# Queries and keys of the second layer by 15 products of two by three by three parts, in two passes of three heads

## The chip, the cores and the metric

The kernel runs on one core of a Trainium2 chip. The metric is device time in microseconds, median of the runs shown. The engines are named as in the profile: PE is TensorE's matmul, PEld its weight load, DVE VectorE, ACT ScalarE, POOL GpSimd, SP the sync engine; SPq is SP's queue, from which every DMA of this kernel is issued.

## The reference

Two layers of graph attention run on 128 graphs of 64 nodes with 768 features, all in float32. What follows is cut to what matters here.

```python
# layer 0: 12 heads of 64, additive attention, gate; then
x = _layernorm(x + layer0(x, adj, ...))
# layer 1: 6 heads of 128
q = _heads(x @ Wq + bq); k = _heads(x @ Wk + bk); v = _heads(x @ Wv + bv)
scores = einsum('bhqd,bhkd->bhqk', q, k) / sqrt(128)
probs = softmax(scores + where(graph_mask, 0, NEG), axis=-1)
ctx = einsum('bhqk,bhkd->bhqd', probs, v)          # heads side by side again
x = _layernorm(x + ctx @ Wf + bf)
```

## The kernel before, in words

The 8,192 tokens are 64 tiles of 128, which are 32 pairs and 16 **quads** of 512 tokens. There are two phases.

**Phase A** (`phase_a`) does layer 0 and the values of layer 1, a pair at a time: `hidden` (h), `gate` (g) and, two pairs late, `value` (v). Each is a product of a 256 x 768 by a 768 x 768 matrix in two by two by two parts with seven products instead of eight (`TURNS`, `by_token`); sums of token blocks (`x_sums`) and of weight blocks (T1 to N4) are made beforehand. Around them `attend` runs the attention of layer 0 on the other engines, each step at a time of its own (`KEYS`). At a pair's end `away` writes x1, transposed, and its four sums to `ops_there` in DRAM, seven blocks in all. In the last pair the matrices of queries and keys are loaded into the places of those no longer needed, and their sums made (`matrix`: four sums in three pieces each).

**Phase B** (`phase_b`) does layer 1, a quad at a time. Its pieces are:

- `queries(q, f)` and `keys(q, f)` for f = 0, 1, 2, each through `by_feature`: seven products of three matmul calls, 128 features by 256 tokens each, which give two heads (f and f + 3) for the quad's 512 tokens. ACT and DVE read the sums out of PSUM into `zone`, with the bias. The operands lie in `zone` as seven blocks, loaded by `load_block` from `ops_there`; the next quad's loads go out as the last keys use the blocks up.
- `slab(Q, f)`: the scores of two heads (s_ps, in PSUM), softmax, the turning of the weights by a copy on ACT, a DMA transpose and two copies back (sT), the context (c_ps), and then for each of two heads a copy into `parts`, a DMA transpose and copies into cT. `parts` has two buffers. In the third slab, right behind the context, `load` issues eight loads of the next quad's values.
- `operands(Q, i)` and `output(Q, i)` for i = 0, 1: the product with Wf for half the tokens of a quad, in two by three by three parts with 15 products (`FIFTEEN`) of two calls each. DVE makes eleven sums of context blocks (sc, L1102) and adds each product to the rows (y, L1148). An accumulator in PSUM is used for several products, and is written on only when the one before has been read.
- `rows_of` loads x1 rows into y, and POOL adds the bias bf; `normed` does the last norm.

The order on each engine is that in which the program emits instructions. It is planned by `Beat`, a clock of the program itself: a product is emitted, its read follows one and a half lengths later, and started lines (`slab`, `operands`, `rows_of`) emit a step whenever their time has come. Every engine works through its own instructions in this order. A quad's three steps f each emit queries, keys and the start of slab f; the output of the quad before follows the keys of f = 1 (i = 0) and of f = 2 (i = 1).

Of the kernel before, what the change touches and what calls it, by code (L numbers as in the profile page):

```python
# [45 lines left out]
F32 = mybir.dt.float32  # L46
# [3 lines left out]
ALU = mybir.AluOpType  # L50
# [24 lines left out]
PLACES = {X11: 0, X12: 1, X22: 2, S1: 3, S2: 4, S3: 5, S4: 6}  # L75

IN_ZONE = {X11: 0, S2: 1, S1: 2, X12: 3, S4: 4, X22: 5, S3: 6}
# [19 lines left out]
    (3, "A5", 3, ((1, 3),)),  # L97
    (1, "A3", 1, ((1, 4),)),
    (0, "2", 11, ((-1, 3),)),
    (4, "14", 2, ((1, 2),)),  # L100
# [5 lines left out]
    (5, "6", 13, ((-1, 4),)),  # L106
    (1, "0", 10, ((1, 5),)),
)

# [99 lines left out]
def two_layers(  # L209
# [68 lines left out]
    def matrix(w, name, engine, gap):  # L278

        t = places[place[name]]  # L280
        blocks = w.rearrange("(k c p) (m n) -> k m p c n", k=2, p=P, m=2)
        for at, k, m in ((W11, 0, 0), (T3, 0, 1), (W22, 1, 1), (W21, 1, 0)):
            for c in range(KH):
                nc.sync.dma_start(t[:, at, c], blocks[k, m][:, c])
                yield gap
        yield 3
        for to, a, b in ((T1, T3, W11), (T2, W22, T1), (T3, W22, T3), (N4, W21, T2)):
            for c in range(KH):
                engine.tensor_tensor(t[:, to, c], t[:, a, c], t[:, b, c], ALU.subtract)
                yield gap  # L290
        ready[f"{name}_sb"] = t
# [85 lines left out]
    ops_there = [dram.tile([P, 2, 7 * KH, P], F32, name=f"ops_there_{q}") for q in range(n_quads)]  # L377
# [3 lines left out]
    zone = const.tile([P, 7 * KH * 2 * P + 8 * P * 2], F32, name="zone")  # L381
# [10 lines left out]
    def load_block(q, k):  # L392

        at = PLACES[k] * KH
        t = in_zone(IN_ZONE[k] * D, KH, 2, P)
        for i in range(2):
            nc.sync.dma_start(t[:, :, i, :], ops_there[q][:, i, at : at + KH, :])
        return t.rearrange("p c i t -> p c (i t)")

    def queries(q, f, blocks, part):  # L400
        quads[q]["qT"] = in_zone(7 * KH * 2 * P, 2, 4 * P)
        by_feature(f"q_{q}_{f}_", blocks, ready["wq_sb"], f, bq_sb, quads[q]["qT"], part)

    def keys(q, f, blocks, part, then=None):
        quads[q]["kT"] = in_zone((7 * KH + 4) * 2 * P, 2, 4 * P)
        by_feature(f"k_{q}_{f}_", blocks, ready["wk_sb"], f, bk_sb, quads[q]["kT"], part, then)

    def by_feature(name, blocks, w, f, b_sb, r, part, then=None):

        sums = [sb(dense[0], [P, BANK], "dense", f"{name}{i}") for i in range(3)]  # L410
        begun = set()
        lo, hi = b_sb[:, f : f + 1], b_sb[:, f + 3 : f + 4]
        T = 2 * P
        u = {}

        def more(i, ps):
            u[i] = part(f"{name}u{i}")[:, 0:T]
            nc.vector.tensor_tensor(u[i], u[1], ps, ALU.add)

        def p1(ps):  # L420
            u[1] = part(f"{name}u1")[:, 0:T]
            nc.scalar.copy(u[1], ps)  # L422

        def p2(ps):
            nc.scalar.activation(r[:, 0, 0:T], ps, AF.Identity, bias=lo)

        def p7(ps):
            nc.vector.scalar_tensor_tensor(r[:, 1, T : 2 * T], ps, hi, u[3], ALU.add, ALU.add)

        def p4(ps):  # L430
            nc.vector.scalar_tensor_tensor(r[:, 0, T : 2 * T], ps, lo, u[1], ALU.add, ALU.add)

        def p3(ps):
            nc.vector.scalar_tensor_tensor(r[:, 1, 0:T], ps, hi, u[2], ALU.add, ALU.add)

        reads = dict(P1=p1, P2=p2, P3=p3, P4=p4, P5=lambda ps: more(3, ps), P6=lambda ps: more(2, ps), P7=p7)
        for what, to, xb, wb in TURNS:
            ps = sums[to][:, 0:T]

            def emit():  # L440
                for c in range(KH):
                    nc.tensor.matmul(  # L442
                        ps,
                        lhsT=w[:, wb, c, f * P : (f + 1) * P],
                        rhs=blocks[xb][:, c, :],
                        start=(c == 0 and to not in begun),
                        stop=(c == KH - 1),
                        skip_group_check=True,
                    )

            read = reads[what]
            beat.product(emit, lambda read=read, ps=ps: read(ps))
            begun.add(to)
            if then:
                then(xb)

    def phase_a(pa, ps_a, dst_pool):
# [25 lines left out]
        w_dst_sb = row(w_dst, "w_dst_sb", pa)  # L485
# [4 lines left out]
        w_src_sb = row(w_src, "w_src_sb", pa)  # L490
        h_b_sb = row(h_b, "h_b_sb", pa)
# [17 lines left out]
        h_of_tile = [pa.tile([P, H0, EP], F32, name=f"h_{i}") for i in range(3)]  # L509
        hx_of = [pa.tile([P, 6, EP], F32, name=f"hx_{i}") for i in range(2)]  # L510
# [299 lines left out]
        def sums_of_pair(p, begin):  # L810
# [12 lines left out]
            def away():  # L823
                there = ops_there[p // 2][:, p % 2]
                nc.sync.dma_start(there[:, 0 : 2 * KH], xo[:, 0:2].rearrange("p k c t -> p (k c) t"))
                nc.sync.dma_start(there[:, 2 * KH : 3 * KH], xo[:, 3])
                nc.sync.dma_start(there[:, 3 * KH : 7 * KH], so.rearrange("p k c t -> p (k c) t"))
# [26 lines left out]
        for p in range(n_pairs):  # L854
# [15 lines left out]
            if p + 1 == n_pairs:  # L870
                beat.start(matrix(wq, "wq", nc.gpsimd, 0.6), 7)
                beat.start(matrix(wk, "wk", nc.vector, 0.6), 14)
# [6 lines left out]
        def first_blocks():  # L879
            for _, _, xb, _ in TURNS:  # L880
                blocks[xb] = load_block(0, xb)
                yield 1

        beat.start(first_blocks())
        value(n_pairs - 2)
        beat.until(lambda: len(blocks) == 7)
        beat.until(lambda: "wq_sb" in ready)
        queries(0, 0, blocks, part)
        beat.until(lambda: "wk_sb" in ready)
        keys(0, 0, blocks, part)  # L890
# [16 lines left out]
    def phase_b(pb, ps_b):  # L907
        bf_sb = row(bf, "bf_sb", pb)


        wf_sb = places[place["wf"]].rearrange("p a b c -> p (a b c)")[:, 0 : 15 * 2 * THIRD]
        wf_sb = wf_sb.rearrange("p (a c n) -> p a c n", a=15, c=2)

        def last_matrix():
            blocks = wf.rearrange("(c k p) (m n) -> k m p c n", k=3, p=P, m=3)
            for k in range(3):
                for m in range(3):
                    nc.sync.dma_start(wf_sb[:, 3 * k + m], blocks[k, m])
                    yield 1
            yield 4  # L920
            for m in range(3):
                last_bias(m)
                yield 1
            ready["bias"] = bf_sb

            for to, a, b, op in (
                (9, 0, 7, ALU.add),
                (10, 5, 8, ALU.add),
                (11, 3, 7, ALU.subtract),
                (12, 3, 8, ALU.subtract),  # L930
                (13, 4, 7, ALU.add),
                (14, 1, 2, ALU.subtract),
                (1, 1, 4, ALU.add),
                (1, 1, 9, ALU.add),
                (4, 14, 13, ALU.add),
# [318 lines left out]
```

## Time and profile before

| | |
|---|---|
| median of 3 runs | 2865.06 us (2863.92 to 2869.85) |
| the profiled execution's own time | 2868.3 us |
| its span, first to last instruction | 2866.4 us |
| mean granted TensorE clock | 0.994 |
| PE busy, phase A 100 to 1300 us | 1198.80 of 1200 us |
| PE busy, phase B 1600 to 2750 us | 1141.88 of 1150 us |
| DVE, ACT, POOL busy, 1600 to 2750 us | 661.10, 399.93, 136.01 us |
| one quad of phase B, 2401.60 to 2490.30 us | 88.7 us, PE busy 87.91, DVE 51.55, ACT 30.90, POOL 10.75 |
| last product of the keys to the end | 2806.94 to 2866.4 us |

Busy time on an engine that is not the bottleneck costs nothing by itself. A group's line names the source line, the engine, the operation, what is written and read, the count, the busy time, the mean length, and the idle time in front with what ended it. A float32 matmul call shows as two PE instructions.

### The profile page before, as it was taken

Reading aid. Unit: us, or ns where it says so; the run is one execution under the profiler, and the core shown is the slowest. Engines: PE = TensorE matmul, PEld = TensorE weight load, DVE = VectorE, ACT = ScalarE, POOL = GpSimd, SP = SyncE. Lnnn points to the kernel's source line nnn. Section 1 sums busy time; section 2 is a strip of 40 time slices with the busy share of each in tenths; the row PEclk is TensorE's granted clock in tenths of the full one; section 3 lists DMA queues with packets and bytes.
Section 4 is the critical chain, followed back from the end, with each engine's and each line's share of the span. In section 5 each row is a group of like instructions: output and inputs, shape, how many; then the busy total and the mean of one; then the engine's idle time right before and its main releaser. Section 6 shows DMA issues by size and latency. Waiting matters only on the chain.

```text
span 2866.4 us, 43840 instructions
## 1 busy us (share of the span) xinstructions
PE 2804.1 (98%) x16168; PEld 2038.1 (71%) x16168; DVE 2039.1 (71%) x4103; ACT 1305.3 (46%) x1562; POOL 1067.2 (37%) x938
## 2 busy tenths in 40 slices
PE   7899999999999999999899999999999999999998
PEld 4455555555555555555588888888888888888886
DVE  6888888888888888888636555565555655556556
ACT  2655655665665665665423333333333333333331
POOL 6656656666665665665421101101011110110102
PEclk9999999999999999999999999999999999999999
DMA  6666666666666666667764445534355343554532
GB/s 205 152 175 170 175 168 169 179 165 170 182 163 172 179 165 170 186 160 193 195 156 116 106 100 131 135 87 117 86 130 135 90 120 84 127 135 94 128 82 63
DMA packets 627014, 409.61 MB, mean 143 GB/s; under 512 B 440176, under 2 KB 573040, under 8 KB 626800
## 3 DMA queue, kind: packets, MB, share of 16 engines
q1 hardware_dynamic: 626800, 406.81, 55.2%
q8 instruction: 128, 2.10, 0.3%
q14 instruction: 86, 0.70, 0.1%
HBM read 186.69 MB, written 119.93 MB: 107 GB/s over the span
## 4 chain that ended last, share of the span: by engine, by line
PE 89%; DMA 4%; DVE 2%; SPq 1%; ACT 1%; issue 1%; POOL 0%; POOLq 0%; ACTq 0%; DVEq 0%
PE v L346 15%; PE o L1135 15%; PE h L346 14%; PE g L346 14%; PE q L442 14%; PE k L442 12%; PE f_all L742 2%; PE s_ps L991 2%; PE c_ps L1047 2%; DMA out<-y 2%; DMA sT<-parts 2%; SPq L980 1%; ACT cT L1069 0%; PE bias_ps L951 0%; DMA s<-parts 0%
## 5 line engine op out<-in xcount | busy, mean ns | idle before, releaser
L370 POOL TENSOR_TENSOR rs<-rs,power 128x1 f32<-128x1 f32 x128 | 73.9, 577 | 1079.4 <-DVE rs L368 1079.4
L346 PE MATMUL h<-w,zone 128*128 128x384 f32 x1320 | 446.2, 494 | 21.7 <-ACT h L533 12.5
L442 PE MATMUL q<-zone,w 128*128 128x256 f32 x2016 | 461.6, 384 | 3.8 <-issue 1.2
L346 PE MATMUL g<-w,zone 128*128 128x384 f32 x1320 | 441.3, 489 | 4.4 <-DVE gate L587 3.3
L442 PE MATMUL k<-zone,w 128*128 128x256 f32 x2016 | 443.2, 379 | 0.9 <-ACT k_u L422 0.9
L442 PEld LDWEIGHTS q<-zone,w 128*128 128x128 f32 x2016 | 381.2, 191 | 63.5 <-issue 8.4
L442 PEld LDWEIGHTS k<-zone,w 128*128 128x128 f32 x2016 | 382.9, 190 | 53.4 <-ACT k_u L422 1.3
L346 PEld LDWEIGHTS h<-w,zone 128*128 128x128 f32 x1320 | 250.7, 192 | 194.6 <-ACT h L533 13.7
L346 PEld LDWEIGHTS g<-w,zone 128*128 128x128 f32 x1320 | 247.5, 190 | 176.4 <-DVE gate L587 12.8
L1135 PE MATMUL o<-w,sc 128*128 128x256 f32 x1364 | 326.7, 384 | 4.7 <-DVE sc L1102 4.7
L1148 DVE TENSOR_TENSOR y<-y,o 128x256 f32<-128x256 f32 x512 | 206.7, 415 | 126.7 <-PE o L1135 120.1
L1135 PEld LDWEIGHTS o<-w,sc 128*128 128x128 f32 x1364 | 256.1, 191 | 43.8 <-DVE sc L1102 6.0
L346 PE MATMUL v<-w,x_sums 128*128 128x384 f32 x768 | 258.5, 486 | 1.7 <-DVE x_sums L315 1.7
L1118 POOL TENSOR_TENSOR y<-y,bf_sb 128x768 f32<-128x768 f32 x64 | 118.4, 1865 | 342.4 <-DMA y<-x_there 313.9
L662 POOL TENSOR_TENSOR bc_e<-th_d,w_dst_sb 128x768 f32<-128x768 f32 x64 | 120.0, 1875 | 287.2 <-ACT th_d L557 267.6
L346 PEld LDWEIGHTS v<-w,x_sums 128*128 128x128 f32 x768 | 145.7, 190 | 104.0 <-DVE x_sums L315 3.0
L1161 ACT ACTIVATE y<-y,rs 128x768 f32<-128x768 f32 x64 | 65.7, 1026 | 157.8 <-POOL rs L371 157.8
L657 POOL TENSOR_SCALAR zone<-zone 128x768 f32<-128x768 f32 x64 | 137.3, 2146 | 0.0
L1009 ACT ACTIVATE s<-s 128x512 f32<-128x512 f32 x48 | 30.1, 626 | 226.2 <-DVE s L1007 226.2
L1102 DVE SCALAR_TENSOR_TENSOR sc<-cT 128x256 f32<-128x256 f32 x217 | 113.9, 525 | 22.9 <-ACT cT L1069 22.8
L650 ACT ACTIVATE gate<-gate 128x768 f32<-128x768 f32 x64 | 53.9, 843 | 166.8 <-DVE gate L593 118.5
L733 ACT COPY bc_e<-th_d 128x1536 uint16<-128x1536 uint16 x64 | 123.2, 1926 | 13.2 <-DMA th_d<-bc_e 13.2
(162 smaller groups left out, 4625.1 us busy)
## 6 DMA issues: line engine op xcount, KB each, us to landing
zone<-ops_there SPq DMA_DIRECT2D x224, 192.0 KB, 4.4
zone<-in_xT SPq DMA_DIRECT2D x32, 768.0 KB, 6.2
zone<-in_x SPq DMA_DIRECT2D x64, 384.0 KB, 3.9
bc_e<-there SPq DMA_DIRECT2D x128, 192.0 KB, 3.4
x_there<-mix SPq DMA_DIRECT2D x64, 384.0 KB, 4.2
ops_there<-x_sums SPq DMA_DIRECT2D x32, 768.0 KB, 3.3
v_there<-v SPq DMA_DIRECT2D x128, 192.0 KB, 2.6
v<-v_there SPq DMA_DIRECT2D x128, 192.0 KB, 3.9
```

Source lines behind the costliest of these rows:

```text
L346: nc.tensor.matmul(ps, lhsT=blocks[xb][:, c, :], rhs=w[:, wb, c, :], start=(c == 0 and to not in begun), stop=(c == KH - 1), skip_group_ch ...
L370: nc.gpsimd.tensor_tensor(rs[:, 0:1], rs[:, 0:1], power, ALU.pow)
L442: nc.tensor.matmul(ps, lhsT=w[:, wb, c, f * P : (f + 1) * P], rhs=blocks[xb][:, c, :], start=(c == 0 and to not in begun), stop=(c == KH - 1),
L657: nc.gpsimd.tensor_scalar(xs, xs, 1.0, None, ALU.add)
L662: nc.gpsimd.tensor_tensor(bc, th, w_dst_sb, ALU.mult)
L733: nc.scalar.copy(halves(e), by_halves(d))
L742: nc.tensor.matmul(f_all[b * N : (b + 1) * N, at : at + E0 + 1], lhsT=e[rows, hd // 2 * P + b * N : hd // 2 * P + (b + 1) * N], rhs=(h[row ...
L1102: nc.vector.scalar_tensor_tensor(s[:, k], of[a], sign, of[b], ALU.mult, op)
L1118: nc.gpsimd.tensor_tensor(y, y, bf_sb, ALU.add)
L1135: nc.tensor.matmul(ps, lhsT=of[xb][:, c, :], rhs=wf_sb[:, wb, c, :], start=(c == 0 and not begun), stop=(c == 1), skip_group_check=True,)
L1148: nc.vector.tensor_tensor(part_of, part_of, ps, ALU.add if sign > 0 else ALU.subtract)
L1161: nc.scalar.activation(y, y, AF.Identity, bias=rs[:, 1:2], scale=rs[:, 0:1])
```

## The change

Queries and keys are now made like the output: with the 15 products of `FIFTEEN`, two by three by three parts. The two parts are halves of a quad's tokens (256 each), the three are the thirds of 256 input features and of the output features. A pass (`one_pass`) gives one head of each third for all 512 tokens, so that two passes c = 0, 1 replace the three steps f. A product is two calls, 128 features by 256 tokens.

- The results are summed up in `zone` itself: the first product of a head writes, with the bias (ACT, or DVE for two of the six), and later ones are added by DVE.
- x1 alone goes to DRAM (`x1T_there`). The eleven sums of a quad's operands (`TOKEN_SUMS`, 128 x 512 each) are made in phase B by `operand_sums`: nine on POOL and two on DVE, during the last output product of the quad before. For quad 0 it is done in the last pair of phase A, for quad 1 on DVE from copies loaded early.
- `matrix` now makes 15 sums of weights for each of the three matrices.
- `FIFTEEN` is reordered at three places, and five accumulators replace six. `FRESH` names the products that begin one.
- The order of a quad is queries 0, keys 0, queries 1, output 0 of the quad before, keys 1, output 1 of the quad before. Slab 0 starts behind keys 0; slabs 1 and 2 both start behind keys 1 and go on into the next quad. The context of the third slab is emitted among the first products of the next quad's queries 1.
- `parts` has one buffer instead of two, cT three instead of four, y's bias comes in two halves, and several constants and tiles of phase A move into `zone`.

```diff
-    (3, "A5", 3, ((1, 3),)),
+    (4, "14", 2, ((1, 2),)),
...
-    (4, "14", 2, ((1, 2),)),
+    (3, "A5", 3, ((1, 3),)),
...
-    (5, "6", 13, ((-1, 4),)),
+    (2, "6", 13, ((-1, 4),)),
...
+FRESH = ("3", "A2", "12", "14", "A5", "6")
+PASSES = (((0, 0), (3, 1), (1, 2)), ((2, 0), (4, 3), (5, 1)))
+SLABS = ((0, 1), (2, 3), (0, 1))
...
+    def operand_sums(q, engines, gap, free=0, early=None, used=None):
+        for i, (name, sign, a, b, op) in enumerate(TOKEN_SUMS):
...
+                while there.get(a) != q or there.get(b) != q:
+                    yield gap
...
+            engine = engines[i > 5]
+            if engine is nc.vector or sign < 0:
+                nc.vector.scalar_tensor_tensor(operand(name), of[0], sign, of[1], ALU.mult, op)
+            else:
+                engine.tensor_tensor(operand(name), *of, op)
+            there[name] = q
+            yield gap
...
+    def one_pass(what, q, c, w, b_sb, then=None):
+        sums, begun = {}, set()
+        for at, xb, wb, to in FIFTEEN:
+            beat.until(lambda: there.get(xb) == q)
+            fresh = xb in FRESH
...
             def emit():
-                for c in range(KH):
+                for i in range(2):
                     nc.tensor.matmul(
                         ps,
-                        lhsT=w[:, wb, c, f * P : (f + 1) * P],
-                        rhs=blocks[xb][:, c, :],
-                        start=(c == 0 and to not in begun),
-                        stop=(c == KH - 1),
+                        lhsT=w[:, wb, i, c * P : (c + 1) * P],
+                        rhs=operand(xb)[:, i, :],
+                        start=(i == 0 and fresh),
+                        stop=(i == 1),
...
+            def read(ps=ps, to=to):
+                for sign, b in to:
+                    m, n = divmod(b, 3)
+                    head, at = PASSES[c][n]
+                    r = heads_of[what][:, at, m * 2 * P : (m + 1) * 2 * P]
+                    if b not in begun and b in (0, 3):
+                        nc.vector.tensor_scalar(r, ps, float(sign), b_sb[:, head : head + 1], ALU.mult, ALU.add)
+                    elif b in begun:
+                        nc.vector.tensor_tensor(r, r, ps, ALU.add if sign > 0 else ALU.subtract)
+                    else:
+                        nc.scalar.activation(r, ps, AF.Identity, bias=b_sb[:, head : head + 1], scale=float(sign))
+                    begun.add(b)
+            beat.product(emit, read, SHORT)
...
-            yield 1
+            yield (1, 5, 13)[f] if q + 1 < n_quads else 1
             nc.vector.tensor_tensor(s3, s3, per_head(m, N), ALU.subtract)
...
-                    parts = sb(pb, [P, BANK], "parts", f"parts_{q}_{f}_{r}", 2)
+                    parts = sb(pb, [P, BANK], "parts", f"parts_{q}_{f}_{r}", 1)
                     nc.scalar.copy(by_halves(parts), halves(c_ps[:, r].rearrange("p i t -> p (i t)")))
                     nc.sync.dma_start_transpose(turned.bitcast(U16).rearrange("p (g t) -> p g t", t=P), parts.bitcast(U16))
-                    yield 1
-                yield 3
+                    Q["slabs"] = f + r
+                    yield 3
+                yield 1
...
+            if before:
+                beat.start(rows_of(before, 1))
+            if q and now:
+                queries(q, 0)
+            if before:
+                beat.start(operands(before, 0))
+            if q and now:
+                keys(q, 0)
+            if now:
+                if q + 1 < n_quads:
+                    load_mask(quads[q + 1])
+                beat.start(slab(Q, 0), 0.8)
+                queries(q, 1)
+            if before:
+                if not now:
+                    beat.start(operands(before, 1), 5)
+                output(before, 0)
+                before["out"] = True
+            if now:
+                if before:
+                    beat.start(operands(before, 1))
...
+                keys(q, 1, then)
+                beat.start(slab(Q, 1), 0.8)
+                beat.start(slab(Q, 2), 5)
+                if following and before:
+                    beat.start(operand_sums(q + 1, (nc.gpsimd, nc.gpsimd), 0.7))
+                beat.start(rows_of(Q, 0), 3)
+            if before:
+                output(before, 1)
+            elif now:
+                beat.until(lambda: Q["scores"] == 3)
             before, Q = Q, quads.get(q + 1)
```

## The prediction

> **What bounds the kernel now.** I read the page's busy times first, then the chain that ended last, then the costliest groups, and then the timelines of PE, SP and ACT around one hand-over between two stages.
>
> ```profile
> PE 2804.1 (98%) x16168; PEld 2038.1 (71%) x16168; DVE 2039.1 (71%) x4103; ACT 1305.3 (46%) x1562; POOL 1067.2 (37%) x938
> ...
> PE 89%; DMA 4%; DVE 2%; SPq 1%; ACT 1%; issue 1%; POOL 0%; POOLq 0%; ACTq 0%; DVEq 0%
> ...
> L442 PE MATMUL q<-zone,w 128*128 128x256 f32 x2016 | 461.6, 384 | 3.8 <-issue 1.2
> L442 PE MATMUL k<-zone,w 128*128 128x256 f32 x2016 | 443.2, 379 | 0.9 <-ACT k_u L422 0.9
> ...
> L1148 DVE TENSOR_TENSOR y<-y,o 128x256 f32<-128x256 f32 x512 | 206.7, 415 | 126.7 <-PE o L1135 120.1
> ```
>
> TensorE bounds both phases: it is busy 98% and carries 89% of the chain. The lines of queries and keys show no idle time to speak of before them, so columns taken away there count in full, if nothing new is waited for. One call in the source shows as two instructions (16 quads x 3 x 21 calls = 1,008 for the queries, shown as 2,016). In the timeline, 42 instructions of k take 9.06 us from start to start of what follows, 0.2157 us each; so a call is 0.431 us.
>
> The next lines are one hand-over: PE, SP's queue, ACT (start, length, what).
>
> ```profile
> 2206.18 1.10 PE L1047 MATMUL c_ps<-v,sT 64*64 64x128 f32 x32
> 2206.69 5.23 SPq L980 DMA_DIRECT2D v<-v_there  x8
> ...
> 2212.65 1.86 SPq L1062 DMA_TRANSPOSE s<-parts  x1
> ...
> 2216.84 1.25 SPq L1062 DMA_TRANSPOSE sT<-parts  x1
> ...
> 2207.35 1.93 ACT L1061 COPY parts<-c_ps 128x1024 uint16<-128x1024 uint16 x2 [0.59 <-PE c_ps L1047]
> ...
> 2217.26 1.39 ACT L1069 COPY cT<-s 128x512 uint16<-128x512 uint16 x2 [4.19 <-DMA s<-parts]
> ...
> 2221.56 1.39 ACT L1069 COPY cT<-sT 128x512 uint16<-128x512 uint16 x2 [2.91 <-DMA sT<-parts]
> ```
>
> After a quad's third slab, SP issues eight loads of the next quad's values (5.2 us) before the two transposes of the result; each transpose is used 4.6 to 4.7 us after its issue begins. The finished context is there 16.7 us after c_ps began. Today nobody notices: its reader, the output products, starts some 35 us after c_ps (in the next quad c_ps is at 2294.4 and the first output product at 2330).
>
> **What the Trainium skill says.** "TensorE: Matmul & The Clock Gate", section on the architectural detail of the array: ScalarE, VectorE and GpSimdE are strict first-in-first-out queues. The trace agrees: the ACT line at 2217.26 waits 4.19 us and what follows it waits too. "DMA: Bandwidth & Descriptors", anatomy of one DMA: a semaphore wait is made on the issuing sequencer, before dispatch, so a blocked issue holds all later ones on SP; the eight loads ahead of the transpose show the same order. "GPSIMD Engine Reference", specifications: GpSimd shares its SBUF interfaces with VectorE and collides with vector instructions that have two SBUF inputs. Here the trace shows it too:
>
> ```profile
> 2091.67 3.78 POOL L1118 TENSOR_TENSOR y<-y,bf_sb 128x768 f32<-128x768 f32 x2 [8.38 <-DMA y<-x_there]
> ...
> 2093.69 0.41 DVE L418 TENSOR_TENSOR k_u<-k_u,k 128x256 f32<-128x256 f32 x1
> 2094.02 1.71 DVE L1102 SCALAR_TENSOR_TENSOR sc<-cT 128x256 f32<-128x256 f32 x1
> ```
>
> The read with one operand in PSUM keeps its 0.41 us, the sum of two SBUF operands goes from 0.42 to 1.71.
>
> **Part by part.**
> 1. Products. Before, a quad takes 6 x 21 = 126 calls of 256 columns for q and k; after, 4 passes x 15 x 2 = 120. 6 x 16 x 0.431 = **41.4 us less**, all on the path.
> 2. Reading the sums out. Per quad DVE goes from 6 x 5 = 30 reads to 4 x 12 = 48, ACT from 12 to 16. At 0.34 us from start to start (415 ns long, overlapping) 18 reads are 6 us of DVE; it is busy 51 us of a quad's 88. This is hidden, as long as no single queue is blocked: a bank is written again after two other products, 1.73 us, and the read takes 0.5 to 0.7 with its hand-over.
> 3. Sums of a quad's operands, 11 of 128x512: nine on POOL at 1.3 us (row L943, 1301 ns), two on DVE at some 0.7 (row L1007, two SBUF operands of that size, 684 ns), up to 1.5 beside POOL. POOL does 11 us of 88 now, so 12 more fit. They follow the loads at the end of the keys and have 15 us of output products as cover; the last six need be there only well inside the next queries. Two DVE sums wait for POOL, with reads behind them: 0 to 1.5 us a quad, I take 0.6. The before kernel's own stall of s_ps on ACT (9.3 us in 11 places) goes, 0.6 a quad: these two cancel.
> 4. DMAs. 12 loads of 128 KB replace 14 of 192 KB per quad; phase one writes x1 once and no sums. SP issues less; worth nothing, as no wait of PE on them is seen beyond 0.9 us.
> 5. **The moved reader.** In the new order the third slab's c_ps stands after two products of the second query pass, and the first output product stands right behind that pass. From c_ps to there PE has 1.04 + 13 x 0.863 + 1.08 (s_ps) = 13.3 us. The chain needs: value loads out at 5.8, s<-parts used at 5.8 + 4.6 = 10.4; then, because `parts` has one buffer instead of two, the second copy (1.01) waits for that landing: 11.4; sT<-parts 3.0 (the shortest landing in the trace) to 4.7: 14.5 to 16.2; ACT cT 0.76; DVE's first sum 0.42: 15.7 to 17.4. PE waits 2.4 to 4.1 us. If the first transpose too landed in 3.0, it would be 0.8. I take 2.6. ACT, blocked in the second copy till 11.4, also delays the read of the tenth product, but that falls inside the same wait. Then the fourth output product needs the sum "11", which DVE has in its order behind the read of the third product: 0.42 + 0.42 + hand-over against no cover, 0.9 (bounds 0 and 1.2). Together 3.5 (0.8 to 5.3) in each of 15 quads: **+52 us** (12 to 80). What waits behind it: all of PE; nothing else is late then, the later waits gain slack.
> 6. First quads and the change of phase. Thirty weight sums of 1.3 us on POOL (seven on DVE) replace twelve of 0.97 on POOL and twelve on DVE. PE already stands 6.7 us there for an ACT copy; the first sums need to be there by the same moment. Between quads 0 and 1 two scores stand back to back. -3 to +10, I take +3.
> 7. The end. Two slabs instead of one come after the last keys, under one output pass (13 us). Slab 1 goes through both DMA transposes with the single `parts`: some 30 us from the last key product to the fourth output product, which needs it, against 25 us now (2806.9 to 2831.9); DVE and POOL then make 22 sums in competition. 0 to +13, I take +7.
>
> Sum: -41.4 + 52 + 3 + 7 = **+21 us**. The profiled execution took 2868.3 us (span 2866.4 and 1.9 around it), 3.2 above the median of 2865.06. 2868.3 + 21 = 2889 in that execution's terms; on the median I state **2886 us**.
>
> **Rivals.**
> - *The wait stays under cover* (this one ends faster): the second transpose lands in 3.0, the first sooner than now because no output row stands in front of it. For: in the slabs without value loads a landing was 3.0 to 4.1. Against: the value loads are still in front, and the second copy still waits. At 1 us a quad: -41.4 + 15 + 5 = -21, 2844 us; it decides below (41.4 - 10) / 15 = 2.1 us a quad. With no wait at all, 2824 to 2834.
> - *DVE or POOL become the bound in the last output pass*: 16 reads, two large sums, two score slabs and a norm come to 12.8 us in 15.1, and with POOL's adds beside them to 15 or more. Each us over is a us of PE. For: 1.71 against 0.42 above. Against: most reads have PSUM on one side. At 2 us a quad on top: 2916 us.
> - *Nothing*: gain and waits cancel within 6 us: a wait of 2.1 a quad, 2865.
> - That the products are not saved is ruled out: the instruction order has 78 fewer matmul calls, which is 96 fewer here, and the last bias in 36 calls of half width instead of 18.
>
> **The numbers.** The forecast (slower by the moved reader) 0.60, with DVE's overload on top 0.14, cancelling 0.06, under cover 0.20. 0.2% is 5.7 us, about what a measurement of this kernel can tell from no change. So faster 0.20, same 0.06, slower 0.74. The forecast alone spans 2872 to 2912; the range that leaves out 2 in 10 goes into both neighbours: 2836 to 2924.
>
> **What would show it.** Right: PE idle before the first output product of each quad, released by DVE sc after ACT cT after DMA sT<-parts, 2 to 4 us, 15 times; ACT's second parts copy waiting for DMA s<-parts; q and k groups with 1,920 instructions each at the same length; a period of 87 to 90 us against 88.5. Wrong: a period near 86 with no idle time before o (then the gain is kept), idle time of PE before q or k on DVE or POOL instead (step 2 or 3 was too small), or an end stage longer by over 15 us.

## The result, and the profile after

The changed kernel takes **2944.49 us** (2940.14 to 2946.84, 4 runs) against 2867.45 for the kernel before in the same comparison: ratio 1.026, 95% interval 1.0247 to 1.0274. It is slower, as forecast, but by 77 us instead of 21, and 2944 us lies above the stated range of 2836 to 2924. The profiled execution has a span of 2938.4 us, 72.0 more than before.

From the page of the changed kernel, in the order of the lines shown of before (busy times, the chain, the costliest groups; the last column is the idle time in front of the group and what ended most of it):

```profile
PE 2788.9 (95%) x16012; PEld 2006.3 (68%) x16012; DVE 2172.1 (74%) x4435; ACT 1347.7 (46%) x1630; POOL 1277.5 (43%) x1143
...
PE 82%; DMA 6%; DVE 4%; issue 2%; ACT 1%; SPq 1%; POOL 0%; DVEq 0%; POOLq 0%; ACTq 0%
...
L487 PE MATMUL q<-zone,w 128*128 128x256 f32 x1920 | 440.6, 385 | 36.0 <-ACT zone L506 16.3
...
L487 PE MATMUL k<-zone,w 128*128 128x256 f32 x1920 | 423.2, 381 | 5.2 <-ACT zone L506 4.5
...
L1168 PE MATMUL o<-w,sc 128*128 128x256 f32 x1116 | 292.9, 391 | 38.8 <-DVE sc L1131 33.3
```

The two groups of q and k have 96 instructions fewer each, at the same length, and their busy time falls from 904.8 to 863.8 us. The saving of 41 us is there. But PE now stands 80 us in front of q, k and o, where it stood 9.4 us (3.8, 0.9 and 4.7).

Where in time the loss arises is read from the PE timeline: the start of the first query product of a quad, q(quad, pass), stands behind the same work in both kernels except for the products saved.

| PE reaches | before | after | later by |
|---|---|---|---|
| q(1,0) | 1489.6 | 1528.1 | 38.5 |
| q(2,0) | 1578.9 | 1625.6 | 46.7 |
| q(15,0) | 2732.1 | 2795.1 | 63.0 |
| end of the span | 2866.4 | 2938.4 | 72.0 |

Each quad saves six calls, 2.6 us. With these added back, waiting and what hangs on it cost 41.1 us up to q(1,0), 10.8 in quad 1, 49.9 in the thirteen quads 2 to 14 (3.8 each) and 11.6 from q(15,0) to the end: 113.4 - 41.4 = 72.0. Over two fifths lie at the change of phase and in the first two quads, where the prediction had 3 us.

**The steady quads.** One hand-over in the changed kernel, from the timelines of PE, SP's queue and ACT (start, length, what; in brackets the idle time before):

```profile
2193.70 8.04 PE L487 MATMUL q<-zone,w 128*128 128x256 f32 x36
2203.37 2.86 PE L487 MATMUL q<-zone,w 128*128 128x256 f32 x12 [1.63 <-ACT zone L506]
2207.49 1.13 PE L1168 MATMUL o<-w,sc 128*128 128x256 f32 x4 [1.26 <-DVE sc L1131]
...
2211.25 1.13 PE L1168 MATMUL o<-w,sc 128*128 128x256 f32 x4 [0.90 <-DVE sc L1131]
...
2191.04 5.21 SPq L1015 DMA_DIRECT2D v<-v_there  x8
2196.35 1.27 SPq L1103 DMA_TRANSPOSE s<-parts  x1
2202.97 1.23 SPq L1103 DMA_TRANSPOSE sT<-parts  x1
...
2201.93 1.01 ACT L1102 COPY parts<-c_ps 128x1024 uint16<-128x1024 uint16 x1 [5.16 <-DMA s<-parts]
```

This is step 5 as it was drawn: value loads first, the first transpose behind them, the second copy waiting for its landing, the second transpose late, the first sum late. ACT's blocked copy also holds the read of the tenth query product (1.63), and the sum "11" costs its 0.90. The stops listed add to 3.8 us; between 2193.70 and 2203.37 lie 9.67 us for 36 instructions of 0.2157, so 1.90 are lost where the line says 1.63. Counted in this way the three stops cost 4.5 us where their lines say 3.8.

**The change of phase.** From the list of VectorE's waits in the changed kernel, 1378 to 1500 us (total, times, longest):

```profile
DVE biasb L1004 <- DMA a8b<-in_adj: 17.5, 2, 13.1
DVE zone L467 <- POOL zone L469: 15.4, 1, 15.4
```

And from PE's list, 1378 to 1530 us:

```profile
PE q L487 <- DVE zone L502: 15.2, 2, 13.0
PE f_all L807 <- POOL zone L469: 10.9, 1, 10.9
PE s_ps L1026 <- DVE s L1037: 6.4, 1, 6.4
PE k L487 <- ACT zone L506: 4.5, 1, 4.5
```

VectorE stands twice at the head of its queue for work of others: 15.4 us in front of an operand sum that needs one of POOL's, and 13.1 us in front of the conversion of quad 1's mask. PE's 10.9 and 13.0 us are their shadows, because the last attention chain (th_d) and the reads of the queries are queued behind. (The list names POOL for f_all, since that came last of several releasers; in e7, which has the same order here, it names VectorE's th_d.) All waits in PE's list add to 46.8 us here and to 13.0 in the kernel before (1340 to 1490 us): 33.8 of the 41.1 us are listed stops, and the rest is time that no line shows.

### The profile page after: what moved, and what is told of

It is laid out like the page before. It is cut to its first block, busy times and chain, and to the rows that moved or that the text cites. A ratio compares the mean times of both kernels' runs of the same rounds, so it can differ in the third digit from the quotient of the medians.

```text
span 2938.4 us, 44261 instructions
## 1 busy us (share of the span) xinstructions
PE 2788.9 (95%) x16012; PEld 2006.3 (68%) x16012; DVE 2172.1 (74%) x4435; ACT 1347.7 (46%) x1630; POOL 1277.5 (43%) x1143
## 4 chain that ended last, share of the span: by engine, by line
PE 82%; DMA 6%; DVE 4%; issue 2%; ACT 1%; SPq 1%; POOL 0%; DVEq 0%; POOLq 0%; ACTq 0%
PE h L391 14%; PE v L391 14%; PE o L1168 13%; PE k L487 13%; PE g L391 13%; PE q L487 10%; DMA s<-parts 2%; PE f_all L807 2%; DMA sT<-parts 2%; PE c_ps L1086 2%; PE s_ps L1026 2%; DMA zone<-x1T_there 1%; DVE zone L467 1%; DVE y L1181 1%; ACT cT L1111 1%
## 5 line engine op out<-in xcount | busy, mean ns | idle before, releaser
L487 PEld LDWEIGHTS q<-zone,w 128*128 128x128 f32 x1920 | 361.7, 191 | 97.9 <-ACT zone L506 21.9
L1168 PE MATMUL o<-w,sc 128*128 128x256 f32 x1116 | 292.9, 391 | 38.8 <-DVE sc L1131 33.3
L1168 PEld LDWEIGHTS o<-w,sc 128*128 128x128 f32 x1116 | 205.5, 191 | 88.2 <-DVE sc L1131 42.9
L727 POOL TENSOR_TENSOR bc_e<-th_d,zone 128x768 f32<-128x768 f32 x64 | 119.7, 1870 | 292.2 <-ACT th_d L622 251.4
L504 DVE TENSOR_TENSOR zone<-zone,q 128x256 f32<-128x256 f32 x320 | 130.8, 417 | 148.3 <-PE q L487 146.1
L469 POOL TENSOR_TENSOR zone<-zone 128x512 f32<-128x512 f32 x130 | 178.5, 1386 | 139.9 <-DMA zone<-x1T_there 118.1
L504 DVE TENSOR_TENSOR zone<-zone,k 128x256 f32<-128x256 f32 x320 | 130.3, 420 | 116.0 <-PE k L487 100.3
L1168 PE MATMUL o<-w,cT 128*128 128x256 f32 x768 | 194.1, 382 | 0.4 <-DVE y L1181 0.4
L1102 ACT COPY parts<-c_ps 128x1024 uint16<-128x1024 uint16 x94 | 94.9, 1009 | 210.4 <-PE c_ps L1086 123.9
L1150 POOL TENSOR_TENSOR y<-y,w 128x384 f32<-128x384 f32 x128 | 137.1, 1093 | 108.6 <-DMA y<-x_there 93.3
L506 ACT ACTIVATE zone<-k,bk_sb 128x256 f32<-128x256 f32 x128 | 60.6, 473 | 245.7 <-PE k L487 245.3
```

The source lines that it names most:

```text
L469: engine.tensor_tensor(operand(name), *of, op)
L487: nc.tensor.matmul(ps, lhsT=w[:, wb, i, c * P : (c + 1) * P], rhs=operand(xb)[:, i, :], start=(i == 0 and fresh), stop=(i == 1), skip_grou ...
L504: nc.vector.tensor_tensor(r, r, ps, ALU.add if sign > 0 else ALU.subtract)
L506: nc.scalar.activation(r, ps, AF.Identity, bias=b_sb[:, head : head + 1], scale=float(sign))
L727: nc.gpsimd.tensor_tensor(bc, th, w_dst_sb, ALU.mult)
L1102: nc.scalar.copy(by_halves(parts), halves(c_ps[:, r].rearrange("p i t -> p (i t)")))
```

## Experiments

A ratio is that to the kernel before, timed beside the run. Its interval is mostly about 0.14% of the time to each side (4 us), so single effects at the change of phase are read from the mark q(2,0) of the profiled execution, one for each run: 1625.6 in the changed kernel. The runs e3, e4, e7 and e10, which leave the change of phase alone, have 1622.1 to 1627.1, so a difference of less than some 4 us in this mark says nothing.

| run | median, us | ratio (95%) | q(2,0) | q(2,0) to q(15,0) |
|---|---|---|---|---|
| before | 2866.78 to 2869.97 | 1 | 1578.9 | 1153.2 |
| changed kernel | 2944.49 | 1.026 (1.0247 to 1.0274) | 1625.6 | 1169.5 |
| e3_parts2 | 2918.88 | 1.0185 (1.017 to 1.02) | 1626.4 | 1148.1 |
| e4_vlate | 2944.58 | 1.0281 (1.0263 to 1.0299) | 1627.1 | 1171.4 |
| e10_spacing | 2908.5 | 1.0143 (1.0129 to 1.0156) | 1623.1 | 1139.0 |
| e7_near | 2882.06 | 1.0056 (1.0043 to 1.0068) | 1622.1 | 1115.2 |
| e1_mask | 2938.95 | 1.0252 (1.0237 to 1.0267) | 1617.8 | 1172.4 |
| e6_queue | 2935.03 | 1.024 (1.0226 to 1.0254) | 1615.7 | 1173.8 |
| e2_own | 2942.92 | 1.0269 (1.0254 to 1.0284) | 1628.3 | 1171.5 |
| e5_sums_dve | 2938.73 | 1.0246 (1.0232 to 1.026) | 1625.7 | 1168.5 |
| e9_later | 2938.79 | 1.0246 (1.0231 to 1.0262) | 1624.9 | 1168.5 |
| e12_no_weight_sums | 2925.53 | 1.0196 (1.0182 to 1.021) | 1608.9 | 1173.4 |
| e8_all | 2864.3 | 0.9991 (0.9984 to 0.9997) | 1603.4 | 1114.7 |
| e11_best | 2863.79 | 0.9985 (0.9978 to 0.9991) | 1607.2 | 1115.1 |
| e13_gap | 2857.76 | 0.9962 (0.995 to 0.9975) | 1600.8 | 1115.1 |
| e14_keys_on_dve | 2858.28 | 0.9965 (0.9951 to 0.9978) | 1599.5 | 1115.5 |

### The moved reader: e3, e4, e10, e7

**e3_parts2.**

```diff
-                    parts = sb(pb, [P, BANK], "parts", f"parts_{q}_{f}_{r}", 1)
+                    parts = sb(pb, [P, BANK], "parts", f"parts_{q}_{f}_{r}", 2)
...
-            a8 = sb(pb, [P, 4, N], "a8", f"a8b_{q}", 2, U8)
+            a8 = sb(pb, [P, 4, N], "a8", f"a8b_{q}", 1, U8)
```

> `parts` gets its second buffer back (the space comes from the uint8 mask, which gets one instead of two). Theory A (the second copy waits 5 us for the landing of the first transpose, which makes the second transpose late by that, as the prediction's step 5 has it): the second copy follows the Exp at once, the second transpose lands some 2.5 us sooner, the stalls of q on ACT zone (16.3 us) and most of o on sc (33.3 us) go; what stays is the sum 11, 0.9 us a quad: 15 x 2.5 = -38, between -30 and -45 us. Rival B (the value loads in front of the transposes on SP set the landing, whatever the buffers): -15 to 0 us.

Measured: about 25 us less, 21 of them in the steady quads. That lies between the two theories. The wait of q on ACT is gone, but o still waits twice a quad. PE's waits of e3, 1626 to 2847 us:

```profile
PE o L1168 <- DVE sc L1131: 22.2, 24, 1.2
PE o L1168 <- DVE y L1181: 6.4, 17, 0.6
```

**e4_vlate** moves the loads and leaves the single buffer.

```diff
-            if f == 2 and q + 1 < n_quads:
-                load(quads[q + 1])
             yield 1
...
                     Q["slabs"] = f + r
                     yield 3
+                if f == 2 and q + 1 < n_quads:
+                    load(quads[q + 1])
                 yield 1
```

> The eight value loads of the next quad are issued behind the two transposes of the third slab's context instead of ahead of them; `parts` stays at one buffer. Theory A (the 5.2 us that SP issues these loads stand in front of the first transpose): the first transpose is issued at once, the second copy follows 4 us later, the context is complete some 4 us sooner than now, and only the sum 11 is still waited for: 15 x 2.9 = -43, between -30 and -48 us. Rival B (the single buffer alone decides): -15 to 0 us. Rival C (the values come late for the next c_ps, since they then land some 7 us later): c_ps waits for the DMA of v, and half of the gain or more is lost.

Measured: no gain. The wait of q on ACT (15.0 us in the steady quads) goes here too, but rival C holds. From the PE timeline of e4:

```profile
1946.21 0.99 PE L1086 MATMUL c_ps<-v,sT 64*64 64x128 f32 x16
1947.66 0.44 PE L1086 MATMUL c_ps<-v,sT 64*64 64x128 f32 x4 [0.46 <-DMA v<-v_there]
...
1950.31 3.63 PE L1168 MATMUL o<-w,sc 128*128 128x256 f32 x8
```

The next c_ps comes in pieces, each waiting for its values. From q(2,0) to q(15,0) the contexts take 20.5 us longer than in the changed kernel (60.8 against 40.3), which uses up the gain; o still waits 20.1 us for sc. In the place shown, the eight output instructions behind also take 3.63 us where eight take 1.89 to 2.00 elsewhere. Six beats later was too late; where the loads stand is not free in either direction.

**e10_spacing** and **e7_near** both have two buffers and bring the second copy and the copies into cT forward by two beats. e7 also puts the loads directly behind the second transpose.

```diff
                     Q["slabs"] = f + r
-                    yield 3
-                yield 1
+                    yield 1
+                if f == 2 and q + 1 < n_quads:      # e7 only; in e10 the loads stay behind c_ps
+                    load(quads[q + 1])
+                yield 3
```

> Two buffers of `parts` and the second copy one beat behind the first, so that the copies into cT and the first sums also stand two beats sooner in the queues of ScalarE and VectorE; the eight value loads stay ahead of the transposes on SP. Between it and the run that also moves the loads (2882 us) lies the loads' share; between it and the run with the second buffer alone (2919 us) lies the place in the queues. Theory A (the place in the queues carries most: with the buffer alone o still waited 0.9 us for each of two sums that VectorE had behind its reads): 2885 to 2900 us. Theory B (the loads carry most: the first transpose cannot be issued before 5.8 us after c_ps, and ScalarE stands in front of the copy into cT with reads behind it): 2905 to 2920 us.

> `parts` has two buffers, the second copy follows the first by one beat instead of three, and the eight value loads are issued right behind the second transpose. Theory A (both the buffer and the loads in front of the transposes make the context late, and value loads six beats later as in the run before were too late for the next c_ps): the context is complete some 3 us sooner than with the second buffer alone, the first sums are made before the second query pass ends, o waits less than 0.5 us a quad for sc, and c_ps does not wait for v. Of 49 us of stalls in the 14 steady quads about 8 stay: -38 to -46 us against the changed kernel. Rival B (the values are still late, or VectorE's reads stand in front of the sums whatever comes): as with the second buffer alone, -20 to -28 us.

Measured: e10 lies in the range of its theory B, 30.5 us less in the steady quads than the changed kernel; e7 gains more than either of its theories allowed, 54.3 us in the steady quads and 62 in the median. PE's waits of e10, 1623 to 2834 us:

```profile
PE q L487 <- ACT zone L506: 19.2, 14, 2.4
PE o L1168 <- DVE sc L1131: 3.6, 4, 0.9
```

and of e7, 1622 to 2807 us:

```profile
PE o L1168 <- DVE sc L1131: 3.6, 4, 0.9
```

With the sums earlier in VectorE's queue o no longer waits, but ACT now meets the copy into cT before the landing and holds a read of q in turn; only with the loads out of the way does that end too. One hand-over of e7, from the timelines of PE, SP's queue and ACT:

```profile
2169.27 1.10 PE L1086 MATMUL c_ps<-v,sT 64*64 64x128 f32 x32
...
2172.45 10.63 PE L487 MATMUL q<-zone,w 128*128 128x256 f32 x48
2182.91 1.03 PE L1168 MATMUL o<-w,sc 128*128 128x256 f32 x4
...
2171.48 1.23 SPq L1101 DMA_TRANSPOSE s<-parts  x1
2172.81 1.28 SPq L1101 DMA_TRANSPOSE sT<-parts  x1
2174.14 5.15 SPq L1015 DMA_DIRECT2D v<-v_there  x8
...
2180.11 1.39 ACT L1111 COPY cT<-sT 128x512 uint16<-128x512 uint16 x2
```

The context is finished 12.2 us after c_ps begins instead of some 17, and PE goes from q to o without a stop. A quad takes 85.8 us against 90.0 in the changed kernel and 88.7 before. The second buffer, the earlier copies and the place of the loads gain 21, 31 and 54 us as they come in one upon the other, and the loads moved alone gained nothing (e4): taking away one uncovers the next.

### The change of phase: e1, e6, e2, e5, e9, e12

**e1_mask** moves quad 1's mask ahead of quad 0's value loads; **e6_queue** also issues the early loads from POOL's queue.

```diff
         load_mask(Q)
+        load_mask(quads[1])
         load(Q)
...
-                if q + 1 < n_quads:
+                if q and q + 1 < n_quads:
                     load_mask(quads[q + 1])
...
-                        nc.sync.dma_start(to[:, :, i, :], x1T_there[1][:, i, k // 3, k % 3 * 2 : k % 3 * 2 + 2, :])
+                        nc.gpsimd.dma_start(to[:, :, i, :], x1T_there[1][:, i, k // 3, k % 3 * 2 : k % 3 * 2 + 2, :])      # e6 only
```

> Only the load of quad 1's mask and its conversion on VectorE are moved: they are issued right behind quad 0's, ahead of the eight value loads and the twelve early operand loads, instead of behind them. Theory A (the change of phase was mis-sized: VectorE stands 13.15 us in front of biasb for that mask, with the reads of the queries behind it, and PE stands 12.98 us): the stall of q<-DVE zone at about 1485 us goes and the median falls by 10 to 14 us against the changed kernel, to about 2932. Rival B (the same loads are needed anyway: the next instruction on VectorE or the sums of quad 1's operands wait for the early loads instead): less than 5 us.

> The mask of quad 1 goes first as in the run that did only this, and the twelve early operand loads are issued from POOL's DMA queue instead of SP's (POOL has nothing to do from 1447 to 1500 us). Theory A (what takes the place of the mask's wait is SP's queue: the transpose of the first slab's weights, s<-sT, stands behind these loads, and ACT waits 6.62 us for it, with the read of the keys behind): k no longer waits for ACT zone in k(0,1) (5.6 us), and the median is 5 to 9 us below the run with the mask alone, that is 10 to 14 below the changed kernel. Rival B (the loads come late from POOL's queue, and the sums of quad 1 wait for them): no better than the mask alone, -5, or slower.

The queue that decides, from the timeline of SP in the changed kernel:

```profile
1460.31 6.20 SPq L670 DMA_DIRECT2D v_there<-v  x4
1468.28 0.33 SPq L1002 DMA_DIRECT2D a8b<-in_adj  x1
1468.66 5.72 SPq L1015 DMA_DIRECT2D v<-v_there  x8
1474.74 1.92 SPq L1214 DMA_DIRECT2D early<-x1T_there  x4
1476.70 4.50 SPq L1214 DMA_DIRECT2D early_sc<-x1T_there  x8
1481.25 0.47 SPq L1002 DMA_DIRECT2D a8b<-in_adj  x1
```

Twenty loads stand in front of the mask of the next quad. Moving it takes 13.0 us of waiting away, but the mark comes only 7.8 us sooner and the median 5.5, between the two theories. The rest went into the next item of that queue: in e1 the transpose s<-sT is issued at 1483.18, behind the early loads and four loads of wf; ACT waits 6.62 us for it, and k waits 5.6 us for ACT. With the early loads elsewhere (e6) the mark is 9.9 us sooner than in the changed kernel, but ACT still waits 5.57 us for the same transpose and k 4.5 us for ACT at that place (9.0 in two places), so the second half of its theory A is not shown. The ratios alone hardly tell either run from the changed kernel: the intervals overlap.

**e2_own, e5_sums_dve, e9_later** move quad 0's operand sums.

```diff
-                beat.start(matrix(wk, "wk", "k c", [nc.gpsimd, nc.vector], 0.7), 14)
+                beat.start(matrix(wk, "wk", "k c", [nc.vector], 0.7), 14)      # e2
...
-                beat.at(begin + 21.8, lambda: beat.start(operand_sums(0, (nc.gpsimd, nc.vector), 0.8, begin + 29.5)))
+                beat.at(begin + 21.8, lambda: beat.start(operand_sums(0, (nc.gpsimd, nc.gpsimd), 0.8, begin + 29.5)))      # e2
+                beat.at(begin + 21.8, lambda: beat.start(operand_sums(0, (nc.vector, nc.vector), 0.8, begin + 29.5)))      # e5
+                beat.at(begin + 23.2, lambda: beat.start(operand_sums(0, (nc.vector, nc.vector), 0.8, begin + 29.5)))      # e9
```

> At the change of phase, POOL makes the weight sums of the queries and nine of quad 0's operand sums, VectorE alone all weight sums of the keys; before, both kinds were dealt out to both engines in turn. Theory A (VectorE stands 15.37 us in front of a sum that needs POOL's, with the last attention chain of the first phase behind it): that idle time of VectorE falls below 5 us, the stall of f_all (10.87 us) to the 6.7 us of the kernel before or less, the ones that follow in q(0,0) and k(0,0) shrink, and the median falls by 10 to 19 us. Rival B (POOL has more to do than the time allows, whoever waits: 15 weight sums and now 9 operand sums of 1.3 us): PE waits for POOL before q instead, and the change is between -5 and +5 us.

> At the change of phase all eleven of quad 0's operand sums are on VectorE (two were there of the first six, and five of the last; POOL had four), nothing else is changed. In the changed kernel and in the run that kept two of them on VectorE, VectorE stands in front of the sum named 12, which needs POOL's sum 3, and POOL has that behind its weight sums; the last attention chain, which f_all waits for, is queued behind it on VectorE. Theory A (this one hand-over makes the stall): VectorE's 15.4 us of idle time before L467 go, f_all waits for 7 us or less, and the median falls by 8 to 16 us. Rival B (VectorE has no room, or stands next before the weight sums that it shares with POOL): -4 to +4 us.

> Quad 0's operand sums at the change of phase are all on VectorE and begin 1.4 beats later, so that they stand in VectorE's queue behind the two operations of the last attention chain on th_d instead of ahead of them; nothing else is changed. With all of them on VectorE but at the old place, VectorE still stood 5.7 and 5.1 us in front of sums whose operands had not landed. Theory A (the place in VectorE's queue is what delays f_all): th_d is made some 13 us sooner, at about 1382 us, f_all's stall of 10 us goes nearly whole, and the median falls by 8 to 14 us against the changed kernel. Rival B (the first query products then wait for the same sums, which are no sooner): 0 to -5 us.

None of them gains anything that can be told. In e2 the two sums with a minus sign stay on VectorE, so the hand-over from POOL was still there: VectorE's 15.4 us and the 10.9 of f_all are unchanged. In e5 VectorE stands before its second and third sum, 5.7 and 5.1 us: for a landing, and then until 1393.83, 0.03 us after POOL's gate operation L723 has ended, which used the place in `zone` that the sum writes. The profile names a DMA there; that L723 is the cause is read from these times and the places, and e9's trace names L723 in front of the same sum. f_all waits 10.4. In e9 the chain is ahead of the sums, and f_all no longer stops PE. From e9, the timelines of PE and POOL:

```profile
1396.54 7.18 PE L391 MATMUL v<-w,x_sums 128*128 128x384 f32 x12 [10.04 <-POOL x_sums L885]
...
1379.07 10.79 POOL L334 TENSOR_TENSOR w<-w 128x512 f32<-128x512 f32 x7
...
1395.02 1.47 POOL L885 TENSOR_TENSOR x_sums<-x_even 128x384 f32<-128x384 f32 x1
```

The same ten microseconds now stand before v, for sums of x that POOL has behind seven weight sums. A wait of ten microseconds keeps its length and changes its name. Behind it in the changed kernel and in e9 is POOL's queue; in e5 it is that queue for one half and a DMA landing for the other.

**e12_no_weight_sums.**

```diff
-        for i, (to, a, b, op) in enumerate(WEIGHT_SUMS):
+        for i, (to, a, b, op) in enumerate(WEIGHT_SUMS if name == "wf" else ()):
```

> The changed kernel without the thirty weight sums of queries and keys (their products then use what lies in those places; loads, operand sums, products and reads stay). It prices what these sums cost at the change of phase. Theory A (POOL's and VectorE's queues are filled by them, 23 of 1.27 us on POOL, and the sums of x, of the operands and the last attention chain stand behind): the stalls of f_all (10.9 us) and v (3.4), and those of q that follow (6), go for the greater part, k's 4.5 and the two later waits (13.0 and 6.4) stay: -15 to -25 us. Rival B (the operand loads and sums themselves are late): -8 to 0 us.

Measured: 19 us less in the median, the mark 16.7 us sooner. Theory A holds in its amount: the wait of v is gone, f_all's is halved (5.5) and the early ones of q fall from 6.0 to 1.2. This prices the sums as a whole: their places in both queues, and what two engines at work in SBUF cost each other. The groups by line on POOL show the added work, before (1340 to 1420 us):

```profile
L289 POOL TENSOR_TENSOR w<-w 128x384 f32<-128x384 f32 x12 | 12.6, 1073 | 0.0
```

and in the changed kernel (1340 to 1440 us):

```profile
L334 POOL TENSOR_TENSOR w<-w 128x512 f32<-128x512 f32 x23 | 32.3, 1419 | 4.9 <-DVE w L334 4.5
L469 POOL TENSOR_TENSOR zone<-zone 128x512 f32<-128x512 f32 x4 | 6.6, 1670 | 0.0
```

POOL has 26 us more to do in the same stage. None of the lists of PE's waits at the change of phase, in any run, names a weight sum: PE does not wait for their results, but for what stands behind them.

### Together: e8, e11, e13, e14

e8 is e6 + e5 + e7 with quad 1's operand sums on POOL instead of VectorE; e11 has e9's place for quad 0's sums instead of e5's; e13 is e11 with

```diff
-                beat.start(matrix(wq, "wq", "k c", [nc.gpsimd], 0.5), 7)
+                beat.start(matrix(wq, "wq", "k c", [nc.gpsimd], 0.8), 7)
```

and e14 is e13 with the keys' weight sums all on VectorE.

> Everything together: quad 1's mask first, the early loads from POOL's queue, quad 0's operand sums on VectorE, quad 1's on POOL, two buffers of `parts`, the second copy one beat behind the first and the value loads right behind the second transpose. Theory A (the waits are separate and add up): 2944 - 42 - 12 - 12 - 5 = 2873 us, between 2860 and 2888, that is within some 20 us of the kernel before on either side. Rival B (each wait that is taken away at the change of phase brings the next one forward): 2944 - 42 - 10 = 2892 us or more.

> The run with everything together (2864 us), with quad 0's operand sums behind the operations on th_d as in this call's first run. Theory A (f_all's stall of 7 us is still there in it and goes): 2854 to 2860 us, faster than the kernel before by 7 to 13 us. Rival B (the next wait at the change of phase comes forward instead): 2862 to 2867 us, as without it.

> The run with everything together and the sums behind th_d (2864 us); in addition the weight sums of the queries are issued every 0.8 beats instead of every 0.5, so that POOL meets the sums of x of pair 14 after five of them instead of after thirteen. Theory A (POOL's order decides: in that run v waits 6.9 us for these sums of x, and they stand behind seven weight sums): this wait goes, the first query products wait somewhat for the last weight sums, net -4 to -9 us: 2855 to 2860. Rival B (the weight sums are the bound whatever the order: q waits for them as long as v did before): within 3 us of 2864.

> As the run before, and the fifteen weight sums of the keys are all on VectorE (POOL had eight of them), so that POOL makes the ten that are left of the queries without a break. Theory A (POOL is the bound of this stage): the last query weights are there some 8 us sooner, and it gains 3 to 8 us on the run before. Rival B (VectorE, with eleven operand sums, reads and the last attention chains, becomes the bound): no gain, or a loss up to 8 us.

e8 keeps what e7 won and comes to q(2,0) 18.7 us sooner; in it the wait of s_ps (6.4 us, for quad 1's five operand sums on VectorE ahead of the scores) is 0.8. It is 0.1% below the kernel before and in the range of its theory A, but not by its terms: 55 us in the steady quads instead of 42, and 22 at the change of phase, counted from the changed kernel, instead of 29. e11 gains nothing on e8: its rival B holds, v waits for the sums of x. The line of PE's list in e11, and POOL's timelines at this place, of e11 and then of e13:

```profile
PE v L391 <- POOL x_sums L885: 6.9, 1, 6.9
...
1379.08 10.46 POOL L334 TENSOR_TENSOR w<-w 128x512 f32<-128x512 f32 x7
...
1395.14 1.44 POOL L885 TENSOR_TENSOR x_sums<-x_even 128x384 f32<-128x384 f32 x1
...
1379.39 1.00 POOL L885 TENSOR_TENSOR x_sums<-x_even 128x384 f32<-128x384 f32 x1
```

e13 only spaces the weight sums of the queries, so POOL's order changes: the sums of x come 16 us sooner, that wait goes, the mark comes 6.4 us sooner, and the kernel takes 2857.76 us, 0.38% below the kernel before (0.25 to 0.50%): **a version that beats both**, by a small amount that is clear of the interval. So POOL's order counts, and not only the amount. e14 moves work off POOL and is the same as e13 within the intervals: theory A of that run is not borne out.

## Why the prediction was wrong, step by step

- **Step 1, the products (-41.4).** Right: 41.0 us of busy time.
- **Step 2, the reads (0).** In e7, with all reads in place, PE waits in the steady quads for 3.6 us of sc and 0.2 of a read, and for nothing else: VectorE has the room. Right.
- **Step 3, operand sums against the stall that goes (0).** Close: e7's 85.8 us a quad stand against 88.7 - 2.6 - 0.66 (the old stall of s_ps, 9.3 us in 14 quads) = 85.5. What was cancelled against 0.6 is 0.3, so this step gains some 5 us in 15 quads. The rival of an overloaded VectorE or POOL falls by the same run.
- **Step 4, the DMAs (0).** Wrong at one place: it counted the loads of a steady quad and not the twelve early ones of quad 1, nor what stands behind them on SP. There they cost 8 to 10 us (e1, e6), which is counted in step 6 below.
- **Step 5, the moved reader (+52).** Right in mechanism and place. e7 takes it away and gains 4.2 us a quad, 63 in 15. The listed idle time of the steady quads is the 3.5 a quad that was forecast, though the 2.6 before the first output product came as two stops, 1.63 in q and 1.26 in o; the rest is what a stop costs beyond its line. The place of the copies among the beats, worth 9 us between e3 and e10, was not in the step. The rival that the wait stays under cover found nothing in the trace. (Its sum takes 5 us for steps 6 and 7, which the steps put at 10; it should have read 2849 instead of 2844.)
- **Step 6, first quads and change of phase (+3, at most +10). This is the step that failed:** it measures 41.1 up to q(1,0) and 10.8 less the moved reader's 3.8 in quad 1, some 48 us. The count was right, thirty weight sums of 1.3 us for twenty-four of less; the mistake was to ask only when their own results are needed. They are needed late. What stands behind them in POOL's queue, the sums of x and of the operands, is needed at once, and what stands behind VectorE's waiting sum, th_d, as well. Leaving the sums out gives 17 to 19 us back (e12), and another order of POOL alone 6 (e13 against e11). The SP queue gives 8 to 10 (e6); the wait of s_ps, 6.4 us, is nearly gone in e8, where only the engine of quad 1's sums was changed for it.
- **Step 7, the end (+7).** Near in the total: 11.6 less the moved reader's 3.8 in quad 15, 7.8 us. Its parts were not near, so the closeness is partly luck: from the last product of the keys to the fourth output product the changed kernel takes 37.1 us (2869.06 to 2906.19), where the step had some 30 against 25. There PE's c_ps waits 6.6 us for ACT's copy into `parts`, and still 4.3 in e7 with two buffers. What follows is 2.3 us shorter than before (32.2 against 34.5).

The sum is then -41.4 - 5 + 63 + 48 + 8, about 72. Of the 51 us between this and the 21 that were forecast, 45 are step 6.

What stays open: added up as if they were independent, the weight sums, the SP queue and the wait of s_ps make 31 to 35 of step 6's 48 us; no run took all three away at once, and e8 and e11 show that such waits do not simply add. e13 still reaches q(2,0) 21.9 us later than the kernel before. Its trace shows waits of q on ACT (10.8 us), whose read stands behind a norm step for which ACT waits 13.7 us (L851, for POOL's rs), and of v on VectorE (7.5 us). No run took these away.

## What to carry to other kernels

Price work that is added to an engine by what is queued behind it, not by when its own result is due: seven sums that nobody needs yet cost ten microseconds, as in e9, if the next in line is needed now. Where one buffer, one row of loads and one place in a queue make a value late together, taking away one showed two fifths of the gain (e3) or nothing (e4); try them together before calling any of them harmless. And a change of phase, which is 5% of the span, deserves the same line-by-line reading of every queue as the loop that is run fifteen times.

## What was not expected of the hardware

After a stop, products ran slower for a while: in the changed kernel twelve instructions of q at 1422.88 us take 4.54 us, where twelve take 2.75 to 2.86 elsewhere, and forty at 1485.12, behind 13.0 us of idle time, take 10.39 instead of 8.6 (40 x 0.2157). The granted clock was 0.73 from 1380 to 1400 us and 0.91 from 1400 to 1425, against 0.95 and 0.83 in the kernel before, which also stops there. The Trainium skill has this in "TensorE: Matmul & The Clock Gate", part 1 on the clock gate: the array's clock falls to half after an idle window of about 3.4 us and comes back after one that is busy. The trace agrees in direction. At one place in e4 eight instructions ran at about half speed (3.63 us, granted clock 0.57 from 1950 to 1954) behind a c_ps in pieces, with four waits that add to 1.43 us, so there no long stop came before it; the other twelve quads of that stage show nothing like it. A stall at the change of phase thus costs more than its line says.

VectorE's sum of two SBUF operands of 128x512 took 0.68 us beside an idle POOL and mostly 1.29 to 1.76 beside a busy one (changed kernel, 1396 to 1425 us). That moving sums to VectorE gains little while POOL still works is argued from these lengths; e5 and e14, which moved some, gained nothing.
